# Local attention with whitening: ScalarE's column copies and weight scalings held back one bank where a half of sums follows

## The chip, the cores and the metric

The kernel runs on one core of a Trainium2 chip. The metric is the device time of one execution in microseconds (us), lower is better. TensorE is called PE in the profile, VectorE DVE, ScalarE ACT, GpSimd POOL, SyncE SP.

## The reference

Two layers follow each other on x, of shape (4, 256, 64, 64), float32.

```python
# layer 0: logits from a dilated 7x7 convolution, then attention over its 49 shifts
k = conv(x, w1, padding=6, rhs_dilation=2) + b1          # 256 -> 128 channels
k = conv(k, w2) + b2                                     # 128 -> 49
attn = softmax(k, axis=1)
shifts = stack([xp[:, :, 2*u:2*u+64, 2*v:2*v+64] for u in range(7) for v in range(7)], axis=1)
y = einsum('bkchw,bkhw->bchw', shifts, attn)
# layer 1: whitening of y in groups of 64 channels over all pixels of all images
Sigma = EPS * I + einsum('gdm,gem->gde', yc, yc) / m     # yc = y minus its mean
# five Newton steps for P, about Sigma ** -0.5; then
out = einsum('gde,gem->gdm', P * sqrt(rTr), yc) * weight + bias
```

## The kernel before

The two convolutions are folded into one with 49 outputs, and the rows and columns of each image are split by parity, so that the dilated convolution is a dense 7x7 one. It is computed by evaluation and interpolation at seven points, in rows and in columns. For image b and row point br, `row_eval` makes a combination `rb` of image rows; `col_ops` makes seven column combinations `xh0` to `xh6` of it; TensorE multiplies them with transformed weights `wr` in three banks, points (1, 2, 0), (3, 4, 6) and (5,) (`BANKS`). "Row (1,4) bank 2" is image 1, row point 4, third bank; its weights are `wr_1_4_2`. Each bank is evicted from `cv` in PSUM to `pv` by ScalarE (L614, and L619 for point 6), and VectorE interpolates `pv` into logits through `zz`. There is one buffer for each `xh` and one for the weights of each bank, and there are two `cv` buffers, which alternate. `ct` and three `rb` are scratch of VectorE's combinations.

For images 1 to 3 the weights are read back from DRAM (`wr<-gd`). In image 1 (and row (2,0)) they are made for the first time: VectorE adds up the taps into `wr`, ScalarE scales it (`scaled`, L481), and SP writes the scaled weights out to `gd` (L482). Two kinds of ScalarE work are put off rather than issued at once: `scaled` together with its write-out, and the copies that make xh0 (L545) and xh6 (L551) from `rb`. They are put on the list `points`, and `conv_bank` empties that list, last in first out, right after it has issued the bank's evictions:

```python
        for waiting in (points, later) if i == 1 else (points,):
            while waiting:
                with tc.high_priority() if waiting is points else nullcontext():
                    copied = waiting.pop()()
```

The logits of an image are transposed and go through softmax (`soft`, `softmax`: exps on ScalarE, L1048, after VectorE's maxima `mx`). `move_terms` copies the terms to `zt` (L1126) and POOL writes them to DRAM (`sd<-zt`, L1145); SP reads them back as diagonal `band` and `bandz` (L1195, L1207). The weighted sum y is TensorE's product of the transposed image, `xb` and `xbz` (`make_blocks`: transposes L1251, copies L1282 and L1273), with the bands (`weighted_sum`, L1320). There are 16 sums n (four in an image), each in two halves, `first_half(n)` and `second_half(n)`. A half stores y to the image's slot (L1342), transposes it (`turn_y`, L1399, copied to `yt` by L1409), and `moments` adds the products for the whitening into `sig` (L1418). The second half of a sum's moments is made in the next `first_half`, or in `finish()` where no half follows at once. `move` then spills a slot that is finished to DRAM (POOL, L1442) and loads the next image in its place (L159).

The order on TensorE is that of the program. The list `steps` of an image has the 18 banks of its rows, with costs 6, 5 and 2, and direct products of cost 12 (`direct_start`, `direct_inf`: acc and cv, L770). Between them are eight gaps (b, j), spread evenly over the cost, and `plan(b, j, f)` puts a half, a `soft` or a `finish` in a gap. So (1,2) to (2,1) hold the halves of image 0, (2,2) to (3,1) those of image 1, and the halves of image 2 start at (3,3). Where a half comes and the bank ahead of it:

```python
            at += cost
            if at * NPC >= (j + 1) * whole:
                gap(b, j)
```

In image 1 that is after bank 1 of rows (1,1) and (1,2), bank 0 of (1,3), (1,4) and (1,5), and bank 2 of (1,5); in images 2 and 3 after bank 1 of rows 0 to 2, then as in image 1. The rest (`rest`) comes after the last bank of image 3. The other engines' order comes from a scheduler that goes by priority and the order of the program.

Of the kernel before, what the change touches and what calls it, by code (L numbers as in the profile page):

```python
# [32 lines left out]
def kernel(  # L33
# [61 lines left out]
    def taps(b):  # L95
        return (0,) if b == INF else (0, 1)

    def pe(ins):
        return tc.keep_in_program_order(ins)
# [34 lines left out]
    def halves(t):  # L134

        return t.rearrange("p c r w -> p c (r w)").rearrange(
            "p c (h r w) -> p c h r w", h=2, r=SH
        )
# [17 lines left out]
    def load_x(s, k, queue):  # L156
        slots[k] = store[s]
        if k in ahead:
            return [queue.dma_start(store[s].rearrange("p c r w -> p (c r w)"), ahead[k])]  # L159
        return [*read_x(halves(store[s]), k, queue)]  # L160
# [85 lines left out]
    for k, c0 in enumerate(range(0, P, CB)):  # L246
        n = min(CB, P - c0)
# [16 lines left out]
    for k0 in range(0, KT, TB):  # L264
        n = min(TB, KT - k0)
# [307 lines left out]
    slot = {}  # L573

    later, points = [], []

    def conv_bank(b, br, i, w):

        if i == 0:
            slot[b, br] = len(slot) % NV if b == 0 else (len(slot) - NV) % 2  # L580
        pts = BANKS[i]
        i0 = sum(len(k) for k in BANKS[:i])
        cv = cv_buf[ncv[0] % 2][:, : 3 * PT].rearrange("p (n q f) -> p n q f", n=3, q=Q9)
        ncv[0] += 1
        if b == 0:
            xv = {bc: xh[bc].rearrange("p (q e f) -> p e q f", e=2 * NCC, q=Q8) for bc in pts}
        else:
            xv = {
                bc: xh[bc].rearrange("p (e g q f) -> p e q g f", e=2 * NCC, g=2, q=Q8)
                for bc in pts  # L590
            }
        for k, bc in enumerate(pts):
            terms = [(sr, sc, cc) for sc in taps(bc) for sr in taps(br) for cc in range(NCC)]
            wv = w[bc].rearrange("p c (a r k) -> p c r a k", r=len(taps(br)), a=NCC)
            for j, (sr, sc, cc) in enumerate(terms):
                for h in range(2):
                    o = cv[
                        h * HB : h * HB + KT, k, sr : sr + Q8, 2 * sc : 2 * (sc + Q8)
                    ]
                    if b > 0:  # L600
                        o = o.rearrange("p q (g f) -> p q g f", g=2)
                    pe(
                        nc.tensor.matmul(  # L603
                            o,
                            wv[:, sc, sr, cc],
                            xv[bc][:, h * NCC + cc],
                            start=(j == 0),
                            stop=(j == len(terms) - 1),
                            skip_group_check=True,
                        )  # L610
                    )
        with tc.high_priority():
            full_ = len(pts) - (INF in pts)
            last = nc.scalar.copy(  # L614
                pv[:K2, slot[b, br], i0 : i0 + full_].rearrange("p n q b -> p (n q b)"),
                cv[:K2, :full_].rearrange("p n q f -> p (n q f)"),
            )
            if INF in pts:
                last = nc.scalar.copy(  # L619
                    pv[:K2, slot[b, br], i0 + full_].rearrange("p q b -> p (q b)").rearrange(  # L620
                        "p (q f) -> p q f", q=Q9
                    )[:, :, : 2 * Q8],
                    cv[:K2, full_, :, : 2 * Q8],
                )
        for waiting in (points, later) if i == 1 else (points,):
            while waiting:
                with tc.high_priority() if waiting is points else nullcontext():
                    copied = waiting.pop()()
                for one in copied if isinstance(copied, list) else [copied]:
                    tc.add_manual_dep(  # L630
                        one.ins,
                        last.ins.name,
                        mybir.DependencyInfo(
                            mybir.DependencyClass.NoSync, mybir.DependencyReason.DATA
                        ),
                        reason="later",
                    )
# [169 lines left out]
    def direct_start(sr):  # L807

        direct(1, 0, sr, conv_psum(), [gr0[:, v, :, sr] for v in range(KS)])
# [604 lines left out]
    def moment(yb, cc, end=False):  # L1414

        for g in range(P // GW):
            pe(
                nc.tensor.matmul(  # L1418
                    sig[g * GW : (g + 1) * GW, cc],
                    yb[:, g, :GW],  # L1420
                    yb[:, g],
                    start=(count[0] == 0),
                    stop=end,
                    skip_group_check=True,
                )
            )
        count[0] += 1

    def moments(n, half):

        for i in range(4 * half, 4 * half + 4):
            for cc in range(NCC):
                moment(ybs[n, i][:, cc], cc)
# [3 lines left out]
    def move(k):  # L1437

        nxt_k = {0: 5, 1: 6, 2: 7}.get(k)
        if nxt_k is not None:  # L1440
            spill[k] = dram.tile([P, NCC * SH * W], F32, name=f"spill{k}")
            dma = nc.gpsimd.dma_start(spill[k], slots[k].rearrange("p a r w -> p (a r w)"))  # L1442
            tc.add_manual_dep(
                dma.ins,
                written[0].ins.name,
                mybir.DependencyInfo(mybir.DependencyClass.NoSync, mybir.DependencyReason.DATA),
                reason="move",
            )
            load_x(k, nxt_k, nc.gpsimd)
# [2 lines left out]

    half_done = {-1}

    def finish():

        n = open_n.pop()
        for t8 in (2, 3):
            turn_y(n, t8)
        moments(n, 1)  # L1460
        if n % 2:
            move(n // 2)

    def first_half(n):
        last = open_n.pop() if open_n else None

        def turn(t8):
            if last is not None:
                turn_y(last, t8)

        def block(t8):
            if (n, (t8, 0)) not in blocks:
                make_blocks(n, t8)

        block(0)
        turn(2)
        weighted_sum(n, 0, 0)
        block(1)
        weighted_sum(n, 0, 1)
        block(2)  # L1480
        weighted_sum(n, 0, 2)
        turn(3)
        weighted_sum(n, 0, 3)
        weighted_sum(n, 0, 4)
        move_terms(n + 1, store_y(n, 0))
        half_done.add(n)
        load_band(n + 1, 0)
        make_blocks(n, 3, y_dve.get((n, 0))) if (n, (3, 0)) not in blocks else None
        if last is not None:
            moments(last, 1)  # L1490
            if last % 2:
                move(last // 2)

    def bands(n, after=None):

        move_terms(n, after)
        if n - 1 in half_done:
            load_band(n, 0)
        if n - 1 in done:
            load_band(n, 1)  # L1500
            move_terms(n + 1, after)
# [22 lines left out]
    NPC = 8  # L1524
    todo, rest = {}, []

    def plan(b, j, *what):
        todo.setdefault((b + j // NPC, j % NPC), []).extend(what)
# [36 lines left out]
    for b in range(B - 1):  # L1565
        for j in range(2) if b else ():
            plan(b + 1, b * j, lambda b=b, j=j: soft(b, j))

    slots[4] = store[4]
    pieces = read_x(halves(store[4]), 4, nc.sync)  # L1570
    for j in range(2, 6):
# [6 lines left out]
    for b in range(1, B):  # L1578

        steps = []  # L1580
        for k, (bk, br) in enumerate(rows):
            if bk == b:
                for i, cost in enumerate((6, 5, 2)):
                    steps.append((cost, lambda k=k, i=i: conv_step(k, i)))
        if b == 1:
            for sr in range(2):
                steps.insert(sr, (12, lambda sr=sr: direct_start(sr)))
            steps.insert(0, (0, lambda: soft(0, 0)))
            steps.insert(3, (0, lambda: soft(0, 1)))
        else:  # L1590
            steps.insert(0, (12, lambda b=b: direct_inf(b)))
        j, at, whole = 0, 0, sum(c for c, _ in steps)
        for cost, f in steps:
            f()
            while rest_of:
                rest_of.pop()()
# [3 lines that stand above are left out]
                j += 1  # L1600
# [26 lines left out]
    n = 4 * last_b  # L1627
# [5 lines left out]
    rest[1]()  # L1633
    move_terms(n + 1)
    rest[2]()
    finish()
    soft_start(1, False)
    move_terms(n + 2)
    for t8 in range(4):
        if (n, (t8, 0)) not in blocks:  # L1640
            make_blocks(n, t8)
    rest[3]()
    rest[4]()
    soft_rows(1, 1)
    for f in rest[5:-2]:
# [167 lines left out]
    for cc in range(NCC):  # L1813
        for b in (3, 2, 1, 0):
# [3 lines left out]
            for k, (r0, nr) in enumerate(rows):  # L1818
# [14 lines left out]
                for pr in range(2):  # L1833
                    o = st[:, :, pr, :].rearrange("p r (h w) -> p h r w", h=2)
                    i = ts[pr][:, : nr * W].rearrange("p (h r w) -> p h r w", h=2, w=SW)
# [48 lines left out]
```

## Time and profile before

| | us |
|---|---|
| median of three runs (lowest, highest) | 682.76 (682.63, 684.98) |
| profiled execution | 683.23 |
| its span in the profile | 681.3 |
| granted TensorE clock in it, share of full speed | 0.996 |
| busy in the span: PE, DVE, ACT, POOL | 648.7, 568.4, 330.4, 117.2 |

The span is the time from the first to the last instruction that the profile shows; the execution's own time has 1.9 us around it. Busy times of engines overlap. Lines of a timeline give the start in us from the span's start, the time in us, the engine, the line, the operation with output and inputs and their sizes, the number of merged instructions, and in brackets how long the engine stood idle ahead of it and what released it.

### The profile page before, as it was taken

The numbers are of one execution on the slowest core, as the hardware profiler recorded it, in microseconds if no ns is written. First come the engines' busy times: TensorE is split into PE (matmuls) and PEld (weight loads), VectorE is DVE, ScalarE is ACT, GpSimd is POOL, SyncE is SP. The second block draws the span as 40 slices with busy tenths as digits, with TensorE's granted clock in tenths as the row PEclk, the third lists the DMA queues.
The fourth block names the chain that finished last, engine by engine and source line by source line (L and its number), as shares of the span: only waits on it lengthen the run. The fifth ranks groups of instructions, "written<-read, shape, count | busy, mean of one in ns | idle before, by whom it ended". The sixth has DMA issues, their size and how long they took to land.

```text
span 681.3 us, 19062 instructions
## 1 busy us (share of the span) xinstructions
PE 648.7 (95%) x7800; PEld 527.3 (77%) x7800; DVE 568.4 (83%) x1248; ACT 330.4 (48%) x857; POOL 117.2 (17%) x177
## 2 busy tenths in 40 slices
PE   6999999999999999999899999999999999999993
PEld 1439573357899998889899998999899989997421
DVE  2699999899489889999999589989998987634773
ACT  1424340023565565566755555373854656534563
POOL 0000551652213020001022020002220203400000
PEclk9999999999999999999999999999999999999998
DMA  8961999992599979322587484026373325648698
GB/s 318 245 162 67 141 280 349 226 182 33 132 198 222 226 156 361 126 69 74 166 270 250 134 297 166 2 67 190 104 190 109 70 63 138 169 101 362 241 391 357
DMA packets 110607, 126.09 MB, mean 185 GB/s; under 512 B 69255, under 2 KB 91896, under 8 KB 109368
## 3 DMA queue, kind: packets, MB, share of 16 engines
q1 hardware_dynamic: 93528, 69.03, 35.2%
q0 software_dynamic: 10944, 37.57, 21.9%
q10 hardware_dynamic: 6048, 18.27, 8.5%
q8 instruction: 61, 1.00, 0.6%
q14 instruction: 26, 0.21, 0.1%
HBM read 78.78 MB, written 52.36 MB: 192 GB/s over the span
## 4 chain that ended last, share of the span: by engine, by line
PE 66%; DVE 20%; ACT 6%; DMA 4%; issue 2%; POOL 0%; ACTq 0%; SPq 0%; DVEq 0%; POOLq 0%
PE cv L603 22%; PE y L1320 11%; PE cv L770 8%; PE acc L770 8%; PE sig L1418 4%; PE tp L1399 3%; PE tp L1251 3%; DVE pv L352 2%; DVE zz L352 2%; PE cv L251 2%; DVE xh L352 2%; DMA out_dram<-out 2%; DVE ct L352 2%; DVE zz L348 1%; ACT d L1048 1%
## 5 line engine op out<-in xcount | busy, mean ns | idle before, releaser
L603 PE MATMUL cv<-xh,wr 128*49 128x128 f32 x4160 | 232.5, 273 | 0.3 <-ACT pv L614 0.2
L603 PEld LDWEIGHTS cv<-xh,wr 128*49 128x49 f32 x4160 | 226.1, 124 | 3.4 <-issue 1.0
L1145 POOL DMA_DIRECT2D sd<-zt x124 | 65.2, 533 | 334.2 <-ACT zt L1126 268.9
L1320 PE MATMUL y<-band,xb 128*128 128x209 f32 x448 | 94.0, 342 | 5.0 <-ACT xb L1282 2.7
L1320 PEld LDWEIGHTS y<-band,xb 128*128 128x128 f32 x448 | 75.7, 190 | 6.5 <-ACT xb L1282 3.3
L614 ACT COPY pv<-cv 113x486 f32<-113x486 f32 (+2 forms) x60 | 26.0, 433 | 86.4 <-PE cv L603 82.2
L352 DVE SCALAR_TENSOR_TENSOR pv<-pv 113x162 f32<-113x162 f32 x176 | 53.4, 325 | 2.1 <-ACT pv L614 1.3
L1126 ACT COPY zt<-d 32x112 f32<-32x112 f32 (+2 forms) x132 | 38.6, 292 | 15.5 <-DVE d L996 9.9
L1409 ACT COPY yt<-tp 128x512 f32<-128x512 f32 x60 | 35.0, 593 | 19.4 <-PE tp L1399 19.0
L1399 PE MATMUL tp<-ident,slot 128*128 128x128 f32 x240 | 41.5, 296 | 1.2 <-ACT slot L1342 1.2
L1048 ACT ACTIVATE d<-tp,mx 128x49 f32<-128x49 f32 x96 | 27.5, 323 | 28.3 <-DVE mx L1045 28.3
L1251 PE MATMUL tp<-ident,slot 128*128 128x128 f32 x256 | 40.5, 282 | 0.0
L1399 PEld LDWEIGHTS tp<-ident,slot 128*128 128x128 f32 x240 | 34.9, 205 | 6.3 <-issue 3.7
L1418 PE MATMUL sig<-yt 128*64 128x65 f32 x1024 | 38.1, 225 | 1.5 <-ACT yt L1409 1.5
L1251 PEld LDWEIGHTS tp<-ident,slot 128*128 128x128 f32 x256 | 38.2, 204 | 0.2 <-issue 0.2
L1418 PEld LDWEIGHTS sig<-yt 128*64 128x64 f32 x1024 | 33.0, 137 | 6.5 <-ACT yt L1409 2.2
L352 DVE SCALAR_TENSOR_TENSOR xh<-ct 128x512 f32<-128x512 f32 x40 | 26.7, 696 | 10.0 <-PE cv L603 9.8
L1282 ACT COPY xb<-tp 128x512 f32<-128x512 f32 x52 | 30.7, 589 | 8.8 <-PE tp L1251 5.6
L770 PE MATMUL acc<-slot,tap 128*49 128x256 f32 (+7 forms) x224 | 34.7, 468 | 0.0
L770 PEld LDWEIGHTS acc<-slot,tap 128*49 128x49 f32 x224 | 16.1, 123 | 17.9 <-issue 15.5
L147 POOL DMA_DIRECT2D slot<-in_x_dram x12 | 20.4, 1699 | 54.6 <-DVE xh L352 38.2
L348 DVE TENSOR_TENSOR pv<-pv 113x162 f32<-113x162 f32 (+1 forms) x77 | 27.7, 369 | 0.3
(259 smaller groups left out, 1144.4 us busy)
## 6 DMA issues: line engine op xcount, KB each, us to landing
out_dram<-out SPq DMA_DIRECT2D x31, 512.0 KB, 5.0
band<-sd SPq DMA_DIRECT2D x64, 242.0 KB, 3.5
sd<-zt POOLq DMA_DIRECT2D x124, 77.0 KB, 3.1
wr<-gd ACTq DMA_DIRECT2D x14, 588.0 KB, 5.2
wr<-gd ACTq DMA_DIRECT2D x14, 490.0 KB, 4.8
slot<-in_x_dram POOLq DMA_DIRECT2D x12, 512.0 KB, 10.4
ahead<-in_x_dram POOLq DMA_DIRECT2D x12, 512.0 KB, 7.7
spill<-slot POOLq DMA_DIRECT2D x3, 2048.0 KB, 10.7
```

The lines of the kernel that those rows point to most:

```text
L348: return in_turn(TT(o, a, b, ALU.subtract))
L352: return in_turn(STT(o, a, f, b, ALU.mult, ALU.add))
L603: nc.tensor.matmul(o, wv[:, sc, sr, cc], xv[bc][:, h * NCC + cc], start=(j == 0), stop=(j == len(terms) - 1), skip_group_check=True,)
L770: nc.tensor.matmul(ps[h * HB : h * HB + KT, :, o0:o1], w[v][:, cc], rhs, start=(j == 0 and k == 0), stop=(j == len(order) - 1), skip_group ...
L1048: nc.scalar.activation(d[:, h, i], t[:, i % NI, h, :KT], AF.Exp, bias=mx[:, i, h : h + 1], accum_out=s[:, h, i : i + 1],)
L1126: ins = nc.scalar.copy(o, i)
L1145: dma = queue.dma_start(bass.AP(tensor=D.tensor, offset=D.offset + h * HS + g * RS, ap=[[LS, TC], [CR * RS, NCH], [1, KS * WS]],), zt[p0 : ...
L1251: nc.tensor.transpose(t[:, h * C + cc * P : h * C + (cc + 1) * P], tile_of(xt, cc, t8, h, pc), turned_by(n),)
L1320: nc.tensor.matmul(y_ps[n, half, cc][:, q0 : q0 + nq, c0:c1], xb[:, cc * P : (cc + 1) * P], rhs, start=(k == 0), stop=(k == len(PIECES[hal ...
L1399: nc.tensor.transpose(t[:, h * C + cc * P : h * C + (cc + 1) * P], tile_of(yt, cc, t8, h, pc), turned_by(n),)
L1409: return nc.scalar.copy(yb.rearrange("p h a g c -> p (h a g) c")[:, :, :GW], t[:, : 2 * C].rearrange("p (e c) -> p e c", c=GW),)
L1418: nc.tensor.matmul(sig[g * GW : (g + 1) * GW, cc], yb[:, g, :GW], yb[:, g], start=(count[0] == 0), stop=end, skip_group_check=True,)
```

## The change

`conv_bank` no longer empties `points` whole where a half of sums or a softmax follows this bank. It issues there only what the bank before kept back, and keeps the rest for the next bank. A flag, set ahead of each step, tells that a gap with something planned follows. Second, the first block pair of sum 0 (four transposes and a copy, `make_blocks(0, 0)`) is planned in gap (1,1), one stretch ahead of `first_half(0)`, and ahead of soft(0,1). Third, in the stretch after the last bank, `finish` for sum 11 (the last of image 2) leaves `moments(11, 1)` to the end of `first_half(12)`, so its 32 `sig` products come after that half's sums.

```diff
     later, points = [], []
+    kept_back, half_next = [], [False]
...
-        for waiting in (points, later) if i == 1 else (points,):
+        due = points[: len(kept_back)] if half_next[0] else points[:]
+        kept_back[:] = points[len(due) :]
+        points[:] = kept_back
+        for waiting in (due, later) if i == 1 else (due,):
             while waiting:
-                with tc.high_priority() if waiting is points else nullcontext():
+                with tc.high_priority() if waiting is due else nullcontext():
                     copied = waiting.pop()()
...
-    def finish():
+    def finish(late=False):
 
         n = open_n.pop()
         for t8 in (2, 3):
             turn_y(n, t8)
-        moments(n, 1)
-        if n % 2:
-            move(n // 2)
-
-    def first_half(n):
+
+        def end():
+            moments(n, 1)
+            if n % 2:
+                move(n // 2)
+
+        return end if late else end()
+
+    def first_half(n, end=None):
...
+        if end is not None:
+            end()
...
+    plan(1, 1, lambda: make_blocks(0, 0))
     slots[4] = store[4]
...
         for cost, f in steps:
+            half_next[0] = (at + cost) * NPC >= (j + 1) * whole and (b, j) in todo
             f()
...
     rest[2]()
-    finish()
+    end = finish(late=True)
     soft_start(1, False)
...
-    rest[3]()
+    rest[3](end)
     rest[4]()
```

In the program that is built, the change reorders these instructions. The xh0 copy of eight rows stands after bank 2 instead of bank 1. The scalings of `wr_1_4_2` and `wr_1_5_2`, with their write-outs on SP's queue, stand after bank 1 of their row instead of after bank 0. The xh6 copies for rows (2,0) and (3,0) and the scaling of `wr_2_0_1` stand after bank 0 of that row. The scheduler moves others with them: the copy `rb<-slot` (L510) of ScalarE now stands ahead of the eviction of row (1,5) bank 0, where it stood between two xbz copies of the half after it; and VectorE's operations around these are interleaved otherwise.

## The prediction

> **What bounds the kernel now.** I read the totals first, then the chain that ended last, then the places where TensorE stands still.
>
> ```profile
> PE 648.7 (95%) x7800; PEld 527.3 (77%) x7800; DVE 568.4 (83%) x1248; ACT 330.4 (48%) x857; POOL 117.2 (17%) x177
> ...
> PE 66%; DVE 20%; ACT 6%; DMA 4%; issue 2%; POOL 0%; ACTq 0%; SPq 0%; DVEq 0%; POOLq 0%
> ```
>
> TensorE is busy 95% of 681.3 us and holds 66% of the chain, so only what makes it wait, or stops it waiting, moves the end. Its waits between 180 and 620 us, from the timeline of PE (start, busy, operation, in brackets the idle time ahead and its releaser):
>
> ```profile
> 191.91 0.97 PE L1320 MATMUL y<-band,xb 128*128 128x209 f32 x4 [1.09 <-ACT xb L1282]
> ...
> 265.22 0.69 PE L1320 MATMUL y<-bandz,xbz 128*128 128x96 f32 x4 [1.11 <-ACT xbz L1273]
> ...
> 293.93 0.97 PE L1320 MATMUL y<-band,xb 128*128 128x209 f32 x4 [0.77 <-ACT xb L1282]
> ...
> 332.66 0.98 PE L1320 MATMUL y<-band,xb 128*128 128x209 f32 x4 [1.39 <-DMA band<-sd]
> ...
> 571.58 1.18 PE L1418 MATMUL sig<-yt 128*64 128x65 f32 x32 [0.25 <-ACT yt L1409]
> ...
> 579.41 0.39 PE L1399 MATMUL tp<-ident,slot 128*128 128x128 f32 x1 [0.80 <-ACT slot L1342]
> ```
>
> Each is about 1 us, most on ScalarE's copies inside a half of sums: the edit aims at these. VectorE has no idle gap from 252.94 to 372.40, so a stall of it there is not made up while TensorE needs its results.
>
> The place that decides is 253 to 268, where bank 2 of row (1,4) follows bank 1. The timelines of ACT, SP's queue, POOL and DVE:
>
> ```profile
> 252.89 0.43 ACT L614 COPY pv<-cv 113x324 f32<-113x324 f32 x1 [2.64 <-PE cv L603]
> 253.22 0.29 ACT L619 COPY pv<-cv 113x144 f32<-113x144 f32 x1
> 253.53 0.68 ACT L545 COPY xh<-rb 128x512 f32<-128x512 f32 x1
> 254.12 0.94 ACT L481 ACTIVATE wr<-wr 128x392 f32<-128x392 f32 x2
> ...
> 254.45 0.57 POOL L1442 DMA_DIRECT2D spill<-slot  x1
> 255.09 2.14 SPq L482 DMA_DIRECT2D gd<-wr  x2
> ...
> 255.09 0.64 DVE L352 SCALAR_TENSOR_TENSOR wr<-rb 128x196 f32<-128x196 f32 x2
> ```
>
> ScalarE evicts the bank, copies a column set and scales two weights; POOL starts the 2,048 KB spill of a slot; SP then writes weights out. The last line, a DVE instruction, begins wr_1_5_2, in the one buffer that held wr_1_4_2, so it follows the last reader of wr_1_4_2: its matmuls and its write-out to DRAM. Before, that write-out is issued at 241.31 and lands in 2.90 us. From the write-outs (L482) of 250 to 262 us, all issued behind the spill:
>
> ```profile
> DMA to landing us min/median/max: 9.5/9.9/10.3
> ```
>
> **The Trainium skill.** DMA: Bandwidth & Descriptors, section "Queues, rings and completion order", says that each DMA engine takes the queues it has work for in turn, a packet at a time; "Issuing engines are not separate DMA queues" says that transfers of sync and gpsimd share the 16 engines. The trace agrees: from 256.5 to 262 each engine alternates one 16 KB spill packet (0.63 us) with one 4.7 KB packet of the write-out (0.18 us). Perfetto Trace Analysis, section "DMA Instruction — HWDGE (DVE, Sync)", says that the completion signal waits for the write's confirmation and can be long after a write to HBM; 2.90 us for a write of 196 KB at a quiet time fits.
>
> **Part 1, first block pair ahead of soft(0,1).** Four transposes (0.74 us, L1251) and one xb copy (0.59) move out of the half at 190. They cost PE the same elsewhere; the wait of 1.09 us ahead of the first sum at 191.91, with 0.16 of smaller gaps behind it, goes. **−1.3.** Soft(0,1)'s exps hide the copy; without that cover it costs 0.6.
>
> **Part 2, copies and scalings held one bank where a half follows.** xh0 copies move one bank later at eight rows; mostly the next user is two banks off and VectorE's work hides the move: 0. Two sorts are different.
>
> (a) wr_1_4_2's scaling lands directly ahead of bank 2 of (1,4). TensorE, which had 11.9 us of slack there, now waits for eviction (0.33+0.31), xh0 (0.60), wr_1_5_0's first scaling (0.47) and wr_1_4_2's (0.53) after 252.89: start 255.2 for 252.67, less a 0.3 gap that it absorbs: +2.2.
>
> (b) The write-out of wr_1_4_2 is now issued by SP ahead of wr_1_5_0's, at about 255.1, some 0.7 us after the spill. It has 1,568 bytes a partition, 8 packets an engine, each behind one spill packet: first packets near 256.7, 8 × (0.63 + 0.07) = 5.6 more, confirmation 0.5 to 1: landing 262.5 to 264, taken 263.5. VectorE reaches wr_1_5_2 at 257.8 (bank 2 ends at 257.2) and stands 5.7 us. Behind it in its order stand the pv combinations and xh5, which row (1,5) bank 2 needs; and in ScalarE's changed order rb<-slot (L510, 1.05 us), which waits for xh5's last operation, stands **ahead** of the eviction of (1,5) bank 0 and of xb_2_1. So: landing 263.5, wr_1_5_2 1.7, xh5 and combinations 1.7, rb 1.05, eviction and zz 0.8, xb_2_1 0.6: y goes on at 269.4 for 262.54, and the 1.11 wait at 265.22 is gone: +5.8, of which part 1 has given 1.3, and (a) lies inside it. TensorE stands **+4.7** at 266.
>
> (c) Bank 2 of (1,5) waits likewise for wr_1_5_2's scaling behind its eviction: 0.43+0.29+0.54 and the start, +1.4. The wait at 293.93 and the 0.16 around it were for ScalarE at scalings that waited for VectorE: −0.9. Bank 1 of (2,0) had 12.3 us for wr_2_0_1; now it waits for eviction 0.56, wr_2_0_2 0.53, xh6 0.6 and the two scalings 0.94 from 304.15, less the four transposes of soft that cover 0.6: +1.7. Sum +6.9 at 316. The two band waits (1.55 + 1.09 at 329 and 331, DMA) absorb 2.7, since the band chain moves less: **+4.2** from 333 on.
>
> (d) The same at image 2 to 3 has no write-out in its way. xh6 of (3,0) and soft(2,1)'s maxima come later, VectorE idles and (3,1)'s xh0, (3,3)'s xh1 and xh0 arrive after TensorE wants them: +0.55, +0.4, +1.2: **+2.15** (slacks were 4 to 6 us at (3,3), all used).
>
> **Part 3, moments(11,1) after first_half(12)'s sums.** 32 sig matmuls (1.18 us) leave the place where they wait for yt (0.25 + 0.16) and stand at 579, where L1399 waits 0.97 for the slot: −0.4 − 1.2 = **−1.6** (−1.0 if the wait is only partly covered).
>
> **Sum.** The profiled execution took 683.23 us (span 681.3 and 1.9 around it); 4.2 + 2.15 − 1.6 = +4.8 gives 688.0. The median of the runs is 0.47 below that execution: **687.6**.
>
> **Rivals.**
> R1, the write-out is not late. If it slips in ahead of the spill, or lands within 2.7 us as at 241.31, VectorE doesn't stand: (b) goes, the 1.11 wait goes and (a) remains; at 333 TensorE stands at −1.0. −1.0 + 2.15 − 1.6 = −0.4: 682.3. This is the rival on the other side, not slower: the mechanism is the landing of gd4<-wr_1_4_2 at (1,4) bank 2, each us of it costs 1 us on TensorE, and it decides at 258. For it: SP's issue is only 0.7 us after POOL's, and the spill's first packets are 1.3 us behind its issue. Against: SP's own were 1.5 behind theirs, so 0.9 us late in all.
> R2, the waits on ScalarE shrink and nothing new takes their place: those in the halves (1.3 at 191, 1.1 at 265, 0.8 at 293, 0.9 at 482, half of it at least) go and part 3 is whole: −4 to −5: 678.5. For: all of these name ScalarE copies, and a held copy is out of their way. Against: the order of instructions puts the scalings directly ahead of their users.
> R3, VectorE's lag of 4.4 us (5.7 less part 1's 1.3) is not absorbed at 329, because the bands come as much later (+2.6), and image 2 to 3 loses 0.6 more: +8: 691. For: VectorE makes the terms that the bands are cut from. Against: the band chain in that stretch hangs on ScalarE's zt copies and POOL's issues, which have 3 us in hand by my reading.
> That the change does nothing can be set aside: the order of the built programs differs at all the places named.
>
> **How the numbers follow.** My forecast 0.50; R1 0.32, R2 0.08, R3 0.10. About 3.4 us (0.5%) is what a measurement of this kernel can tell from no change: below 679.4 is R2; R1 falls within; the forecast's band of landings (262.5 to 264) and of part 3 gives 686.4 to 688.7, a fifth of it within. Faster 0.08, same 0.40, slower 0.52. The range 680.5 to 690.8 takes in R1 with its own 2 us and leaves out R2 and half of R3.
>
> **What would show it.** Right: the first wr<-rb after 257 waits for a DMA for 5 us, the write-out takes 7 to 9 us, (1,5)'s eviction is behind L510, and PE's y in that half waits over 5 us. PE waits of 1.4 to 2.2 at the heads of (1,4) b2, (1,5) b2 and (2,0) b1; none at 191. Wrong: no DVE gap there, or a landing before 259. A gap over 3 us on PE anywhere before 240 or after 400 would be something that I didn't see.

## The result, and the profile after

| | before | after |
|---|---|---|
| median of four runs, us | 682.94 | 689.52 |
| lowest to highest | 682.63 to 684.98 | 688.73 to 690.58 |
| profiled execution, us | 683.23 | 689.54 |
| span, us | 681.3 | 687.7 |
| granted TensorE clock | 0.996 | 0.991 |

The changed kernel is slower: the ratio is 1.0078, 95% interval 1.0054 to 1.0103. The forecast was 687.6, slower. (The experiments below were compared with new runs of the kernel before, whose median was 684.08 us beside e1, e3, e4 and e6, and 683.36 beside e5, e8, e9 and e10; so their ratios say more than their microseconds.)

The page of the changed kernel, first its totals and its chain, then the first of its costliest groups (the column after the bar is busy time and mean ns, then the idle time ahead of the group and what ended most of it):

```profile
PE 650.3 (95%) x7800; PEld 528.6 (77%) x7800; DVE 568.3 (83%) x1248; ACT 331.8 (48%) x857; POOL 117.2 (17%) x177
...
PE 78%; DVE 13%; ACT 4%; DMA 3%; issue 1%; POOL 0%; ACTq 0%; SPq 0%; DVEq 0%; POOLq 0%
...
L604 PE MATMUL cv<-xh,wr 128*49 128x128 f32 x4160 | 233.7, 273 | 7.5 <-ACT wr L481 4.8
```

The same instructions do the same work. What is new is 7.5 us of idle time ahead of the conv banks, 4.8 of it ended by ScalarE's scalings (before: 0.3 us). The line numbers are those of the changed kernel, up to 12 higher.

The place that the prediction named, on SP's queue, POOL, DVE and ACT:

```profile
253.67 4.09 SPq L482 DMA_DIRECT2D gd<-wr  x3
...
253.05 0.57 POOL L1446 DMA_DIRECT2D spill<-slot  x1
...
261.73 0.64 DVE L352 SCALAR_TENSOR_TENSOR wr<-rb 128x196 f32<-128x196 f32 x2 [5.25 <-DMA gd<-wr]
...
265.21 1.05 ACT L510 COPY rb<-slot 128x1024 f32<-128x1024 f32 x1 [7.80 <-issue]
266.57 0.32 ACT L714 COPY zz<-pv 113x144 f32<-113x144 f32 x1 [0.31 <-DVE pv L352]
266.79 0.56 ACT L615 COPY pv<-cv 113x486 f32<-113x486 f32 x1
267.24 0.59 ACT L1286 COPY xb<-tp 128x512 f32<-128x512 f32 x1
```

SP issues the write-out of wr_1_4_2 0.62 us behind the spill. VectorE stands 5.25 us before it may overwrite wr_1_4_2: the write-out lands at 261.63, 8.0 us after its issue (its last packet ends at 260.89). ScalarE reaches the eviction and xb_2_1 only after L510, as forecast.

TensorE's waits, in order, with the ones that answer to those of before:

```profile
190.25 0.98 PE L1324 MATMUL y<-band,xb 128*128 128x209 f32 x4
...
253.70 4.58 PE L604 MATMUL cv<-xh,wr 128*49 128x128 f32 x80 [2.25 <-ACT wr L481]
...
267.88 3.16 PE L1324 MATMUL y<-band,xb 128*128 128x209 f32 x8 [4.44 <-ACT xb L1286]
270.83 1.01 PE L1324 MATMUL y<-bandz,xbz 128*128 128x96 f32 x4
...
278.40 1.96 PE L604 MATMUL cv<-xh,wr 128*49 128x128 f32 x32 [1.14 <-ACT wr L481]
...
312.85 3.37 PE L604 MATMUL cv<-xh,wr 128*49 128x128 f32 x58 [1.40 <-ACT wr L481]
...
465.23 6.32 PE L604 MATMUL cv<-xh,wr 128*49 128x128 f32 x112 [0.92 <-ACT xh L545]
...
495.38 3.70 PE L604 MATMUL cv<-xh,wr 128*49 128x128 f32 x64 [1.06 <-DVE xh L345]
499.84 1.96 PE L604 MATMUL cv<-xh,wr 128*49 128x128 f32 x32 [0.76 <-ACT xh L545]
```

The wait of 1.09 us at 191.91 is gone, as are those at 265, 294, 330, 333 and 579. In their place stand waits at the heads of three banks of images 1 and 2, one of 4.44 us in the half of sum 2, and three in image 3. A wait of 0.89 us inside a half of image 2 (0.86 at 482 before) is still there.

An easier way to see it is the shift of TensorE: the start of a bank in a kernel's profiled execution less its start in that of the kernel before (us, later is positive). The columns to the right are experiments that follow.

| start of | after | 4 KB spill | scalings now | copies now | one hold |
|---|---|---|---|---|---|
| (1,2) b0 | −1.57 | −1.37 | −1.45 | −1.34 | −1.32 |
| (1,4) b1 | −1.39 | −1.20 | −1.28 | −1.32 | −1.33 |
| (1,4) b2 | +1.02 | +1.21 | −1.28 | +1.09 | −1.33 |
| (1,5) b1 | +6.29 | +1.22 | −1.30 | +5.26 | −1.35 |
| (1,5) b2 | +7.67 | +2.53 | −1.30 | +6.57 | −1.35 |
| (2,0) b0 | +6.67 | +1.54 | −1.30 | +5.56 | −1.33 |
| (2,0) b1 | +8.14 | +3.00 | −1.30 | +7.54 | −1.33 |
| (2,1) b2 | +5.29 | +0.15 | −3.97 | +7.00 | −3.43 |
| (2,2) b1 | +5.47 | +0.30 | −2.95 | +7.00 | −3.43 |
| (3,1) b0 | +5.68 | +0.48 | −2.78 | +6.99 | −3.40 |
| (3,3) b1 | +8.01 | +2.81 | −0.46 | +6.96 | −3.41 |
| first y of sum 12 | +6.35 | +1.45 | −2.12 | +5.32 | −5.08 |
| last PE instruction | +6.36 | +1.90 | −1.88 | +6.00 | −3.62 |

At 51 us, ahead of anything that the change touches, the changed kernel's execution already stood at −0.30; so much of such a shift is that execution's own. The last row of "one hold" holds a loss of another kind: between 638 and 641 us of that execution the granted clock was 0.50, which took 1.4 us.

### The profile page after: what moved, and what is told of

Its sections match the earlier page's. It is cut to its first block, busy times and chain, and to the rows that moved or that the text cites. A ratio compares the mean times of both kernels' runs of the same rounds, so it can differ in the third digit from the quotient of the medians.

```text
span 687.7 us, 19066 instructions
## 1 busy us (share of the span) xinstructions
PE 650.3 (95%) x7800; PEld 528.6 (77%) x7800; DVE 568.3 (83%) x1248; ACT 331.8 (48%) x857; POOL 117.2 (17%) x177
## 4 chain that ended last, share of the span: by engine, by line
PE 78%; DVE 13%; ACT 4%; DMA 3%; issue 1%; POOL 0%; ACTq 0%; SPq 0%; DVEq 0%; POOLq 0%
PE cv L604 26%; PE y L1324 13%; PE cv L774 12%; PE acc L774 8%; PE sig L1422 4%; PE tp L1403 4%; PE tp L1255 3%; PE cv L251 2%; DMA out_dram<-out 2%; DVE pv L352 1%; DVE xh L352 1%; PE tp L1720 1%; DMA gd<-wr 1%; DVE d L1000 1%; PE apply L1720 1%
```

## The experiments

**The spill in 4 KB pieces (e3_pack4k).** All instructions stand in the order of the changed kernel; only the spill of slot 0 has another layout in DRAM, in which it also comes back at the end.

```diff
-            spill[k] = dram.tile([P, NCC * SH * W], F32, name=f"spill{k}")
-            dma = nc.gpsimd.dma_start(spill[k], slots[k].rearrange("p a r w -> p (a r w)"))
+            i = slots[k].rearrange("p a r w -> p (a r w)")
+            if k == 0:
+                spill[k] = dram.tile([4, P, NCC * SH * W // 4], F32, name=f"spill{k}").rearrange(
+                    "k p n -> p k n"
+                )
+                i = i.rearrange("p (k n) -> p k n", k=4)
...
+            dma = nc.gpsimd.dma_start(spill[k], i)
```

> The changed kernel, and the order of all its instructions as in it, with one difference: the spill of slot 0 is laid out in DRAM so that it goes in pieces of 4 KB a partition instead of 16 KB (and comes back so at the end). Stall theory (the write-out of wr_1_4_2 shares the DMA engines with the spill packet by packet, and VectorE stands behind its landing): each of its 8 packets an engine now waits 0.16 us and not 0.63, so it lands about 8 x 0.23 + 1.5 + 0.7 = 4 us after its issue instead of 8; VectorE's wait of 5.25 us shrinks to 0.5 to 1.5, TensorE's wait ahead of y after xb_2_1 from 4.4 to under 1.5, TensorE stands near +1 against before at (1,5) bank 1 instead of +6.3. Time 682.5 to 684.5. Rival A (the write-out waits for the spill as a whole, whatever its packets): VectorE's wait stays at 5 us and the time at 689.5. Rival B (the loss is from ScalarE's scalings directly ahead of their banks): VectorE's wait goes but the time stays over 687.

Measured: median 685.13, ratio to before 1.0018 (1.0007 to 1.0028). The timelines of SP's queue, DVE and PE of this kernel:

```profile
253.86 5.17 SPq L482 DMA_DIRECT2D gd<-wr  x3
...
258.18 0.64 DVE L352 SCALAR_TENSOR_TENSOR wr<-rb 128x196 f32<-128x196 f32 x2 [0.51 <-DMA gd<-wr]
...
265.14 1.58 PE L1327 MATMUL y<-band,xb 128*128 128x209 f32 x8
```

The write-out lands at 258.08, 4.2 us after its issue instead of 8.0. VectorE's wait falls from 5.25 to 0.51 us; 1.2 us of that fall is VectorE itself, which comes to the buffer later here, because bank 2 of (1,4) ran in part at half the granted clock. The y sums no longer wait, and TensorE at (1,5) b1 stands at +1.22 instead of +6.29. In the records of DMA packets, the write-out's 128 packets of 1,568 bytes (0.07 us each) go in turn with the spill's: 110 of 16 KB (0.62 us) start among them in the changed kernel, in 5.5 us, and here 180 of 4 KB (0.16 us), in 2.4 us. So the price of the write-out is the packet size of its neighbour. Rival A falls, since the write-out lands while the spill still runs. Rival B falls as the whole of the loss, since the time is below 687, but not as a part of it: the three waits for scalings are still there (+3.00 at (2,0) b1, where the next run stands at −1.30). The time is 0.6 us over the range that I expected, which was set against 682.94 us; the ratio times that is 684.2, inside it. In its trace TensorE stands at +1.57 ahead of the last part of the kernel and 0.33 more come in that; the runs spread from 683.97 to 687.65.

**Scalings never held (e1_scale_now).**

```diff
-        due = points[: len(kept_back)] if half_next[0] else points[:]
-        kept_back[:] = points[len(due) :]
+        kept_back[:] = [
+            f for f in points[len(kept_back) :] if f.__name__ != "scaled"
+        ] if half_next[0] else []
+        due = [f for f in points if f not in kept_back]
```

> The changed kernel, but weight scalings with their write-outs are never held back; only column copies are. Stall theory: the write-out of wr_1_4_2 is issued near 240 again and lands in 3 us, VectorE's 5.25 us wait is gone, and so are the waits at the heads of (1,4) b2 (2.4), (1,5) b2 (1.4) and (2,0) b1 (1.5); what is left of the change is the earlier block pair (-1.3), the later moments (-1.6) and the losses of image 3 from held copies (+2.3): 682 to 683.5. Rival (held copies carry the loss): over 687.

Measured: median 681.51, ratio 0.9971 (0.9960 to 0.9983): faster than the kernel before. All three scaling waits and the stall of VectorE are gone (shifts of −1.28 to −1.30 from (1,4) b1 to (2,1) b1). The rival falls. The time is below the range expected, and the reason is between (2,1) b1 and b2: TensorE goes from −1.30 to −3.97. The two band waits, at 329.83 and 332.66 in the kernel before (the second is shown in the prediction), are gone although TensorE comes **earlier** to them:

```profile
329.83 0.98 PE L1320 MATMUL y<-band,xb 128*128 128x209 f32 x4 [0.93 <-DMA band<-sd]
```

**Copies never held (e6_copies_now).** The same edit with `== "scaled"`.

> The changed kernel, but column copies are never held back; only the weight scalings with their write-outs are. Stall theory: VectorE's wait on the write-out stays at 5 us, TensorE stands at +6 at (1,5) bank 1; the waits of image 3 at (3,1) and (3,3), 2.3 us in all, go, and (2,0) b1 waits 0.6 less: 686.5 to 687.5. Rival (held copies carry the loss): under 684.

Measured: median 689.20, ratio 1.0080 (1.0063 to 1.0098). The stall is there (4.98 us on DVE) and image 3 loses nothing (+6.99 to +6.96), both as the stall theory says, but the time was 1.7 us over its range (0.9 by the ratio). The reason is on PE's timeline:

```profile
339.65 0.98 PE L1326 MATMUL y<-band,xb 128*128 128x209 f32 x4 [2.04 <-DMA band<-sd]
```

TensorE comes 7.5 us later to these bands than in the kernel before, and still waits 2.04 us for one of them; only 0.54 us of the two waits goes (+7.54 to +7.00). Together with the run above: the band waits don't go because TensorE is late; they go because a held **copy** makes the bands early.

**TensorE kept busy in its wait (e4_fill).**

```diff
         block(2)
+        if n == 2:
+            t = tp()
+            for k in range(28):
+                pe(nc.tensor.transpose(t[:, k % 4 * P : (k % 4 + 1) * P], ident, ident))
         weighted_sum(n, 0, 2)
```

> The changed kernel with 28 extra transposes of the identity (some 4 us of TensorE's time, their result is read by nothing) between the last block transposes and the y sums that wait for xb_2_1, so that TensorE stays busy through most of its longest wait. Clock theory (the y sums after the 4.4 us wait ran at half the granted clock, 3.16 us for 8 instead of 1.58, because TensorE had stood still): the granted clock stays at 1.0 through 263 to 273, the 8 y matmuls take about 1.6 us, the bandz ones 0.7, and (1,5) bank 1 starts 1.5 to 2 us earlier than in the changed kernel; the time falls by 0.5 to 2 us, to 687.5 to 689. Rival (they were slow for another reason, the DMA traffic or the landing of operands): they stay at 3.2 us and the time stays at 689.5 or rises.

Measured: median 688.73, ratio 1.0075 (1.0057 to 1.0093). The windows of the changed kernel (busy us of PE, PEld, DVE, ACT and POOL, then the granted clock, DMA share and GB/s):

```profile
263.00:268.00 5.00, 0.56 (x5) 0.37 (x4) 5.00 (x18) 2.46 (x5) 0.00 (x0) 0.80 0.96 341
268.00:270.00 2.00, 2.00 (x6) 1.94 (x7) 1.97 (x5) 1.91 (x5) 0.00 (x0) 0.50 0.96 405
270.00:272.00 2.00, 2.00 (x9) 1.96 (x9) 1.86 (x3) 0.12 (x1) 0.00 (x0) 0.50 0.99 332
```

and those with the extra transposes, followed by their PE timeline:

```profile
263.00:268.00 5.00, 5.00 (x44) 5.00 (x43) 5.00 (x17) 2.69 (x6) 0.00 (x0) 1.00 0.97 348
268.00:270.00 2.00, 2.00 (x16) 2.00 (x15) 1.97 (x4) 1.68 (x4) 0.00 (x0) 1.00 0.99 419
```

```profile
265.04 3.22 PE L1492 MATMUL tp<-ident 128*128 128x128 f32 x28
268.10 1.58 PE L1324 MATMUL y<-band,xb 128*128 128x209 f32 x8
```

With TensorE busy the clock stays at 1.00, at the same DMA load, the 8 y matmuls take 1.58 us instead of 3.16, and (1,5) b1 starts 2.10 us earlier (+4.19 for +6.29). So 2 us of the stall's cost are TensorE at half its clock after standing still. (This execution ran at 0.50 once before, from 254 to 257 behind the wait of 2.24 us at (1,4) b2; the 1.7 us lost there vanish in the wait for xb_2_1.) The profiled executions differ by 2.0 us at the end; the medians by 0.8, with intervals that overlap. The four executions are two pairs: 687.56 and 687.84 us at a mean granted clock of 0.994, and 689.62 and 689.67 at 0.991 and 0.993, while all four of the changed kernel were at 0.990 or 0.991. So in the two longer ones the clock seems to have fallen for longer, at a place that no trace shows, and the median lies between the pairs.

**The two other parts of the change (e8_block, e5_both).** For e8_block, to the kernel before:

```diff
+    plan(1, 1, lambda: make_blocks(0, 0))
```

For e5_both, to the changed kernel, which so holds nothing back:

```diff
-            half_next[0] = (at + cost) * NPC >= (j + 1) * whole and (b, j) in todo
+            half_next[0] = False
```

> The kernel before with the earlier block pair alone. TensorE stands at -1.3 from 192 to 325, and to the end if the band waits at 329 and 331 stay 2.6 us; a ratio of 0.998. Rival: the bands come no earlier and it stands at 0 from 333 on: no change.

> The kernel before with the earlier block pair and the later moments, and no hold at all. By the prediction's steps -1.3 - 1.6 = -2.9 against before if the band waits at 329 and 331 keep their 2.6 us, a ratio of 0.9955 to 0.996. Rival: the band chain does not move with TensorE there and takes the 1.3 back: -1.6, a ratio of 0.9975.

Measured: e8_block 682.62, ratio 0.9984 (0.9970 to 0.9998); e5_both 681.31, ratio 0.9956 (0.9939 to 0.9974). The ratios are those of the first theory; the rivals' (1 and 0.9975) lie just outside the intervals. The traces seem to say the opposite for the block pair: e8_block stands at −1.34 as far as (2,1) b1 and at +0.20 from (2,1) b2 on. Its PE timeline at the bands, and from e5_both PE's timeline and a window of it:

```profile
328.85 0.97 PE L1320 MATMUL y<-band,xb 128*128 128x209 f32 x4 [1.29 <-DMA band<-sd]
...
331.51 1.76 PE L1320 MATMUL y<-band,xb 128*128 128x209 f32 x4 [1.21 <-DMA band<-sd]
```

```profile
331.79 1.52 PE L1324 MATMUL y<-band,xb 128*128 128x209 f32 x4 [1.51 <-DMA band<-sd]
```

```profile
332.00:334.00 2.00, 2.00 (x9) 1.86 (x9) 2.00 (x7) 0.00 (x0) 0.00 (x0) 0.52 1.00 227
```

In e8_block the two band waits take 2.50 us for 2.32 in the kernel before, and the second sum starts 1.15 us earlier: the bands came earlier with TensorE, and the rival falls. What takes the gain back is the clock, which is 0.50 from 331 to 334, so that four y products take 1.76 us for 0.98; e5_both shows the same. Other executions kept the gain: the 10 of 20 of e8_block with a mean clock of 0.995 or more took 682.07 us on average, the 22 of 33 of the kernel before 683.16. The later moments gave 1.64 us in e5_both (from +0.68 at the second half of sum 11 to −0.96 at sum 12), undisturbed.

**One hold (e9_one_hold).** The pair, the moments, and of all holds only xh6 of row (2,0).

```diff
+            f for f in points[len(kept_back) :] if f.__name__ != "scaled" and (b, i) == (1, 2)
```

> The kernel before with the earlier block pair and the later moments, and one hold only: the xh6 copy of row (2,0) waits until after bank 0 of that row (with it VectorE takes both maxima of soft(1,0) ahead of the next row's rb). Theory from the run with scalings never held: this one hold brings the terms of sum 4 to DRAM some 3 us earlier and so removes the two band waits (2.6 us) at 329 to 331 of the kernel before; the other holds of image 2 and 3 cost 1.0 at (2,2) b1 and 2.3 at (3,1) and (3,3) and gain nothing. So -1.3 - 2.6 - 1.6 = -5.5 against before, perhaps +1.0 if the wait at (2,2) b1 belongs to this hold: a ratio of 0.992 to 0.994. Rival (the band waits go for the sum of the holds of image 2, not for this one): -2.9, a ratio of 0.9955 to 0.996, and band waits near 327.

Measured: median 678.39, ratio 0.9907 (0.9883 to 0.9932), faster than both kernels and a little below the range. Its timelines of DVE, SP's queue and PE, and below them lines of DVE and SP's queue of the kernel before:

```profile
303.48 0.57 DVE L1050 TENSOR_REDUCE mx<-tp 128x8 f32<-128x392 f32 x1 [2.23 <-PE tp L1014]
304.41 2.29 DVE L345 TENSOR_TENSOR rb<-rb,rb 128x2048 f32<-128x2048 f32 x1 [0.16 <-ACT xh L551]
306.62 0.34 DVE L1029 RECIPROCAL s<-s 128x8 f32<-128x8 f32 x2
...
323.09 1.00 SPq L1201 DMA_DIRECT2D band<-sd  x2
...
327.74 0.98 PE L1326 MATMUL y<-band,xb 128*128 128x209 f32 x4 [0.17 <-DMA band<-sd]
```

```profile
306.09 0.56 DVE L1044 TENSOR_REDUCE mx<-tp 128x8 f32<-128x392 f32 x1
...
311.18 0.27 DVE L1023 RECIPROCAL s<-s 128x8 f32<-128x8 f32 x2
...
326.51 2.13 SPq L1195 DMA_DIRECT2D band<-sd  x2
```

The next row's `rb` must wait for the held xh6 copy (`[0.16 <-ACT xh L551]`), and soft(1,0)'s second maximum now stands ahead of it in VectorE's order. VectorE idles 2.23 us there, yet the softmax's reciprocal comes at 306.62 instead of 311.18, and SP reads the first bands at 323.09 instead of 326.51. The band waits of 0.93 and 1.39 us become 0.17 and nothing above 0.3. The rival of this run falls. In its trace this hold gains 2.10 us (−1.33 to −3.43).

**No hold in image 3 (e10_not_img3).** The condition is `f.__name__ != "scaled" and b + i // 2 < 3`.

> The changed kernel with scalings never held, and column copies held in images 1 and 2 but not for rows of image 3. If the holds of image 3 alone cost 2.3 us (0.7 at (3,1), 0.6 given back, 2.2 at (3,3)), this is 2.3 us faster than the run with all copies held, -4.2 against before, a ratio of 0.993 to 0.995; the wait of 1.0 at (2,2) b1 stays. Rival: the losses of image 3 come from image 2's changed order, and the time stays at a ratio of 0.997.

Measured: median 679.26, ratio 0.9921 (0.9890 to 0.9952), a little below the range. TensorE's shift stays at −2.78 to −2.81 from (3,0) to (3,3) b1, where it lost 2.32 with image 3's holds (e1_scale_now). So these losses belong to image 3's holds alone. At (2,2) b1 it loses 0.79, waiting for an xh0 copy, which e9_one_hold doesn't.

## Why the prediction was right, and where not

- **The first block pair, −1.3.** Measured −1.57 against −0.30 at the start: −1.27. It came out as forecast. I had not asked whether the band waits at 329 and 331 move with it; e8_block shows that the bands move with TensorE (waits of 2.50 us for 2.32), but that the clock can fall behind those waits and take the gain back.
- **(a), +2.2 at (1,4) b2.** −1.39 to +1.02: +2.41, behind wr_1_4_2's scaling.
- **(b), the write-out behind the spill.** The stall is 5.25 us for 5.7, and the write-out took 8.0 us, where 7 to 9 was named as the sign; VectorE goes on at 261.7, and with the 1.3 us of the pair taken off the forecast 263.5 this was to be 262.2. The y sums went on at 267.88, where 269.4 less 1.3 gives 268.1, after a wait of 4.44 us that was to be over 5. Up to there the chain is right. TensorE at (1,5) b1 was to stand at +4.7 (its terms, 5.8 less 1.3, add up to 4.5) and stands at +6.29. The term that was too small is the step from the y sums to that bank: the matmuls after the wait were priced at their old durations, and they ran at a clock of 0.50. e4_fill puts 2.1 us on that. The 4 KB run shows the cause of the stall: with the write-out 3.7 us quicker the wait at the y sums is gone.
- **(c), +1.4, −0.9, +1.7.** Measured +1.38, −1.00, +1.47, in the places named.
- **"The two band waits absorb 2.7, since the band chain moves less".** 2.85 us went, and the sign and size are right, but the reason is wrong, so the size is luck: this was the step that failed. The bands did move less than TensorE (SP reads the first at 331.72 for 326.51, so +5.2 against +8.1), but not for slack in their chain: without the held copies only 0.54 us went (e6_copies_now). The waits go for the held xh6 of row (2,0), which takes soft(1,0) ahead of the next row on VectorE (e1_scale_now, e9_one_hold). I had seen the changed order of the maxima and not priced it. It is a gain of the change that is there without any stall too: e1_scale_now keeps it and is faster than the kernel before.
- **(d), +2.15 in image 3.** Measured +5.68 to +8.01: +2.33, all of it from image 3's own holds.
- **Part 3, −1.6.** Measured −1.64; sum 12's L1399 at 586 no longer waits for the slot.
- **The sum.** 688.0 was forecast for the profiled execution, 689.54 was measured. The 1.5 us over are the half clock (2.1) and 0.4 of small losses from (2,2) to (2,4), less the 0.45 by which the stall was shorter, the head start of 0.3 and small differences. So the time came near although one term was missing, and the bands came out by a reason that wasn't seen.
- **The rivals.** R1 (no late write-out): fell. The 4 KB run is its case, and there its sum was too low: +0.15 at (2,1) b2 for −1.0 (−0.7, if its terms −1.3, +2.2, −1.1, +2.2 and −2.7 are added up), and a ratio of 1.0018 where 682.3 was 0.999. About 1.4 us of that are half clock again, after the wait of 2.24 us at (1,4) b2 (0.51 from 256 to 258 in that run), so R1 missed the same term as the forecast. R2 (waits shrink and nothing takes their place): fell; the waits at 191, 265 and 293 went as it said, but longer ones took their place. R3 (more lag to the end): fell; TensorE's shift is constant from (2,4) to (3,1), and image 3 lost what was forecast.

The Trainium skill's statement that each DMA engine takes its queues in turn by packets (DMA: Bandwidth & Descriptors, "Queues, rings and completion order") agrees with the 4 KB run: with the neighbour's packets four times smaller the write-out landed 4.2 us after its issue instead of 8.0.

What stays open: where the clock fell in the two longer executions of e4_fill, and how much of the stall's cost would go if L510 stood behind the eviction, which wasn't tried.

## What to carry to other kernels

Moving a put-off step moves its DMAs too: look at which transfers are in flight when each is issued now, since a small write behind a large one with 16 KB packets took 8 us instead of 3, and find who overwrites its source. Holding work back is not one decision: of the holds here one gained 2.1 us in its trace, the copies of image 1 did nothing that shows, and others cost 0.8 us (the copy at (2,2) b1), 2.3 (the copies of image 3) and 8.5 (the scalings, by +7.54 in e6_copies_now against −0.96 in e5_both at (2,0) b1), so try them one at a time. Where a wait goes away in a trace, ask whether the waiter became late or the awaited became early; a run in which the waiter is later still, and waits all the same, tells the two apart.

## What the runs showed of the hardware that was not expected

After TensorE had stood 4.44 us, its granted clock was 0.50 from 268 to 272, and matmuls took twice as long (0.395 us each for 0.198); 28 extra transposes in the gap kept it at 1.00. In e5_both two waits of 0.89 and 1.51 us within 4 us did the same (0.52 at 332 to 334), and in e3_pack4k and e4_fill one of 2.24 us. One of 2.25 us at the same place in the changed kernel, one of 2.04 in e6_copies_now, and two of 0.93 and 1.39 in the kernel before did not: the granted clock behind them was 1.00.

The clock's records in the traces show a part of what tells these apart. Between 20 and 670 us, each stretch at 0.50 in the ten traces is 3.41 us long or twice that, and begins a whole multiple of 3.41 us after the clock first rose to 1.00, at 10 to 12 us. So the clock changes on a grid of 3.41 us, and it matters how a wait lies on it. The waits of 2.24 us lay whole in the one interval ahead of the slow one (251.15 to 254.57 in e3_pack4k, 250.42 to 253.83 in e4_fill); that of 2.25 us was split by the grid at 252.31 into 0.86 and 1.39. A limit doesn't come out of it: 1.68 us of waiting in one interval (e5_both) and 1.95 (e8_block) were followed by half clock, 1.95 in e6_copies_now was not, 1.40 in the changed kernel was not, and 1.17 in the last part of e9_one_hold was, among smaller products.

One such interval at half clock costs at most 1.7 us of TensorE's work, and that is also how the executions of one kernel differ: of the 29 of the kernel before beside e3_pack4k, 14 had a mean clock of 0.995 or more and took 683.28 us on average, 15 had 0.993 or 0.994 and took 685.02. A mean clock that is lower by 0.0025 is what one interval of 3.41 us at half clock makes in 681. After the wait of 4.44 us, which reached into two intervals and was followed by half clock up to 272.8, the cost was 2.1 us, about half as much again as the wait itself.
